# A conditioned transformer block in float32: the second norm turned through DRAM, and a planner's order that counts two engines as taking turns on a port

## Chip, core and metric

One core of one Trainium2 chip. The metric is the device time of one execution in microseconds (us), the median of several runs. The profile is one further execution, taken with the hardware profiler; times read from it are compared with its own time.

Engines are named as the profile names them: PE (TensorE, matrix products), PEld (its weight loads), DVE (VectorE), ACT (ScalarE), POOL (GpSimd) and SP (SyncE, which here only issues DMAs). Each engine works through its own instructions in the order in which they were written.

## The reference

A transformer block on x of 8 x 1024 x 512 in float32, with 16 heads of width 32 and a hidden width of 2048. Six vectors per batch row (shift, scale and gate of both halves) come from the condition.

```
mod = silu(condition) @ Wada + bada
sh_a, sc_a, gt_a, sh_m, sc_m, gt_m = split(mod, 6)
x  = x + gt_a * attention(layernorm(x, g1, be1) * (1 + sc_a) + sh_a)     # causal, with Wqkv, Wproj, bproj
xm = layernorm(x, g2, be2) * (1 + sc_m) + sh_m
x  = x + gt_m * (gelu(xm @ W1 + b1) @ W2 + b2)
```

## The kernel before

**Blocks.** The 8 x 1024 tokens are 16 blocks of 512, numbered 0 to 15: two per batch row. The queries of an even block see their own keys, those of an odd block also the keys of the block before. A block is held as four tiles of 128 tokens.

**Products.** The large products (queries, keys, values, projection, the four "up" parts of W1 and the down product of W2) are done with one Strassen level: seven products of halves in place of eight. The left or right operand of a token block is therefore kept as seven pieces: B11, B21, B22 and T1 are halves of the normed and turned block `xm`, T2, T3 and T4 are sums in a tile `t`. The sums of the weights are made once and kept in DRAM. Each product runs in four column groups of 32 on TensorE (`matmul`, L201). Weights stream in pieces of 256 KB through a ring of nine buffers, in the order in which the plan uses them (`fetch`, L336), on SP's queue. A piece can be loaded when the one nine places earlier was used up.

**The plan.** `plan[w]` (L234 to L269) lists by hand the linear steps that run beside the attention of block w: `load_xr` (x read again as the residual), `proj` (output projection of block n = w - 1, added to the residual), `mt` (second norm and its modulation), `u` (four up parts), `d` (four down parts: seven products and their additions to the residual), and for block w + 1 or w + 2 the queries, keys, values and first norm (`q`, `k`, `v`, `norm_a`, `at`). Down parts that don't fit are carried to the front of the next window in `late`. Before the change these carried parts stand ahead of `v` and `proj`.

**The planner.** While the kernel is being written down, it keeps a clock for each engine (`now`, L94) and the time at which each tile is written or free (`written`, `left`). `note` (L112) advances a clock by a fixed duration. The attention (`attend`, L1824) writes score units, exponent units and weighted sums in order; `step_aside` (L1462) fills the time until an operand is due with steps of the plan, whichever thread is due first. Nothing of this runs on the chip: it fixes the order on each engine. `either` (L154) puts an elementwise operation on VectorE or GpSimd, whichever the clocks say ends first; GpSimd is preferred by a margin of 1500 ns. `note` delays a VectorE operation marked `port` to the end of a GpSimd operation in which it would start; the other way round nothing is delayed.

**The norm.** `normalize` (L617) takes the statistics of four tiles on VectorE, the root and the application (L653) on ScalarE. Then the block is turned, so that features lie on partitions, and scaled and shifted by the modulation (`modulated`, L732). There are two ways. (1) On TensorE: sixteen transposes against the identity (L769) into three shared PSUM banks, and a scaling that reads the bank (L784 on ScalarE or L778 on VectorE). (2) Through DRAM (`turn_rows`, L702): VectorE transposes squares of 32 x 32 (L708), four DMAs write the turned squares to a DRAM tile (L719), one DMA of 1 MB reads them back (L725), and the scaling reads SBUF. `is_turned` (L376) chooses the second way for the first norm of blocks 4 to 15; x is then loaded in an order of rows that makes the tokens come out in sequence. The second norm takes the first way in all blocks.

**Lists of work in waiting.** `jobs` (statistics and square transposes on VectorE) run in sequence when their first entry is due. `transfers` (the writes and the read of a turned block) likewise, by `run_transfers` (L575). The results are stored by `store` (L1189) at once when it is called.

Of the kernel before, what the change touches and what calls it, by code (L numbers as in the profile page):

```python
# [22 lines left out]
def kernel(  # L23
# [72 lines left out]
    shape = [None]  # L96
    pool_spans = []
    NEVER = float("inf")
# [5 lines left out]
    def due(reads=(), writes=()):  # L104
# [5 lines left out]
        return t  # L110

    def note(engine, ns, reads=(), writes=(), port=False):  # L112
# [5 lines left out]
        if engine == "POOL":  # L118
            pool_spans.append((start, end))
# [31 lines left out]

    margin = [1500]

# [47 lines left out]
    def matmul(ps, lhsT, rhs, start, stop, reads=(), bank=None):  # L201

        for j in range(HPG):
            r = slice(j * hd, (j + 1) * hd)
            nc.tensor.matmul(  # L205
                ps[r, :], lhsT[:, r], rhs, start=start, stop=stop, skip_group_check=True
            )
        n = 1
        for d in rhs.shape[1:]:
            n *= d  # L210
        note_pe(2 * COLUMN * n, "columns", reads, [] if bank is None else [("l", bank)])

    MM = 853
# [26 lines left out]
    }  # L240
    late = []
    for w in range(1, NB):
        n = w - 1
        m = mlp_steps(n)
        even = blocks[n][1] == 0
        rows_a = [("rows", blocks[n][0], "a")] if even else []
        rows_m = [("rows", blocks[n][0], "m")] if even else []
        own = m[:1] + ([("load_xa", w + 2)] if w + 2 < NB else []) + m[1:3]
        own += [("norm_a", w + 2)] if w + 2 < NB else []
        if w == NB - 1:  # L250
            steps = late[:1] + [("load_xr", n)] + rows_a + [("proj", n), ("mt", n)] + late[1:]
            steps += [("v", w)] + rows_m + own + m[3:6]
            late = m[6:]
        else:
# [5 lines left out]
            at = [("at", w + 2)] if w + 2 < NB else []  # L260
            if blocks[w][1] == 0:

                late = m[3:4] + at + m[4:]
            else:
                steps += m[3:4] + at + m[4:6]
                late = m[6:]
        plan[w] = steps
    n = NB - 1
    plan[NB] = [("load_xr", n), late[0], ("beside", ("proj", n)), late[1], ("mt", n)] + mlp_steps(n)  # L269

# [103 lines left out]

    SQ = 32

    def is_turned(key):
        return key[0] == "a" and int(key[1:]) >= 4

# [181 lines left out]

    def add_job(job, reads, first=False):

        at = sum(1 for other in jobs if other[2]) if first else len(jobs)
        jobs.insert(at, (job, reads, first))

    def run_jobs(everything=False):
        while jobs and (
            everything or (now["DVE"] <= now["PE"] and due(jobs[0][1]) <= now["PE"])
        ):  # L570
            jobs.pop(0)[0]()

    transfers = []

    def run_transfers(everything=False):  # L575
        while transfers and (
            everything or max(queue_free[0], transfers[0][0]) <= now["PE"]
        ):
            ready, transfer = transfers.pop(0)
            queue_free[0] = max(queue_free[0], now["PE"], ready) + 700  # L580
            transfer()
# [25 lines left out]
    def hurry():  # L607

        while jobs and due(jobs[0][1]) <= now["PE"] + 500:
            jobs.pop(0)[0]()  # L610
        while excursions and due(excursions[0][1]) <= now["PE"] + 500:
            excursions.pop(0)[0]()
# [4 lines left out]
    def normalize(tiles, key, sources):  # L617
# [42 lines left out]
        for t in range(NTT):  # L660
            add_job(lambda t=t: statistics(t), [sources[t]], key[0] == "m")

# [39 lines left out]
    def turn_rows(key, tiles, xm):  # L702

        squares = xm.rearrange("p c (j r) -> p (c j) r", r=P)
        there = kept.tile([D, TB], F32, tag=f"turned_{int(key[1:]) % 2}", name=f"turned_{key}")

        def turn(t):
# [21 lines left out]
        for t in range(NTT):  # L729
            add_job(lambda t=t: turn(t), [("hat", key, t)])  # L730

    def modulated(key, gain, shift, b, guards):  # L732
        for t in ("B11", "B21", "B22", "T1", "T2", "T3", "T4"):
# [15 lines left out]
            "T4": sums[:, 2, :, :],  # L749
        }  # L750
        xm_of[key] = part
        at = {t: (key, t) for t in part}
# [60 lines left out]
    qTs, kTs, vs = {}, {}, {}  # L813
    projected, valued = set(), set()
    xm_of, hTs, hidden = {}, {}, set()
# [80 lines left out]
    def strassen(step, x, dest, target, row, done, put=None, after={}):  # L896
# [14 lines left out]
        def product(a, t, bank=None):  # L911
            start = bank is None
            reads = [(x, t)] + ([("sums", *step, a)] if raw and a[0] == "S" else [])
            for i in range(2):
                for k in range(2):
# [10 lines left out]
                    lhsT, rhs = (second, first) if row else (first, second)  # L926
                    matmul(
                        banks[bank][:, ts(i, HB)], lhsT[:, ts(i, P)], rhs,
                        start and i + k == 0, k == 1, reads, bank,
# [59 lines left out]
        start(tail())  # L989

    def project_T(step, store, pool, tag, done):

        n = step[1]
        dst = pool.tile([P, NC, TB], F32, tag=tag, name=f"{tag}_{n}")
        store[n] = dst
# [27 lines left out]

    residual, stored = {}, {}
    y_count, y_keys = [0], {}
# [69 lines left out]
    def project_out(n):  # L1095
# [8 lines left out]
        begun = []  # L1104

        def begin(t):

            bank = yield from accumulate(
                [(attT[:, c, ts(t, P)], piece(at[c])) for c in range(NC - 1)], [("att", n)], False
            )  # L1110
            begun.append(bank)

        for t, xt in enumerate(tiles):
            if last:
                while len(begun) <= max(t, 1):
# [3 lines left out]
                matmul(  # L1119
                    banks[bank], attT[:, NC - 1, ts(t, P)], piece(at[NC - 1]), False, True,  # L1120
                    [("att", n, t)], bank,
                )
            else:
                bank = yield from accumulate(
                    [(attT[:, c, ts(t, P)], piece(at[c])) for c in range(NC)], [("att", n)]
                )
# [62 lines left out]
    def store(n, t):  # L1189
        b, h = blocks[n]  # L1190
        for i in (2 * t, 2 * t + 1):
            r0 = h * TB + i * P
            nc.sync.dma_start(out[b, r0 : r0 + P, :], residual[n][:, i, :])
        stored[n + 1] = max(stored.get(n + 1, 0.0), due([("xr", n, 2 * t), ("xr", n, 2 * t + 1)]))

    def down(n, part):
# [19 lines left out]
        def product(operand):  # L1216
# [3 lines left out]
            for i in range(NQ):  # L1220
                p = next(at)
                for k in range(2):
                    c = 2 * i + k
                    hT = hTs[n, 2 * kh + c // NC][:, c % NC, tokens]
                    for m in range(2):
# [3 lines left out]
                        else:  # L1229
                            yield [], []  # L1230
                        matmul(
                            banks[bank][:, ts(m, HB)], hT[:, ts(m, P)], halves(p)[:, k, :],
                            c + m == 0, c == 2 * NQ - 1, reads, bank,
# [96 lines left out]
    def perform(step):  # L1330
# [12 lines left out]
        elif kind == "load_xr":  # L1343
            n = step[1]
            b, h = blocks[n]
            if n == NB - 2:
                xr = kvp.tile([P, NTT, D], F32, tag="kT", name=f"xr_{n}")
# [3 lines left out]
            for t in range(NTT):  # L1351
                r0 = h * TB + t * P
                nc.sync.dma_start(xr[:, t, :], x[b, r0 : r0 + P, :])
                landed = max(now["PE"], stored.get(n, 0.0)) + LANDING + 700 * t
                written["xr", n, t] = landed
# [15 lines left out]
        elif kind == "k":  # L1371
            yield [("free for k", step[1])], []
            yield from project_T(step, kTs, kvp, "kT", lambda: None)
        elif kind == "q":
# [449 lines left out]
    def attend():  # L1824
        previous = None
        for n in range(NB):
# [20 lines left out]
            written["free for k", n + 2 if n % 2 else n + 1] = 0.0  # L1847
            written["free for k", n + 1] = 0.0
            for g, k, n_slots, upto in slots:
                if (n, g) == groups[-1]:  # L1850
# [50 lines left out]
    def next_scores():  # L1901
        until(lambda: units[unit_at[0]][0] in projected)
        scores(*units[unit_at[0]])
# [15 lines left out]
    needs += sum(score_need(*unit) for unit in units)  # L1919
    for n in range(NB):  # L1920
        written["attended", n] = NEVER
        written["v done", n] = NEVER
# [30 lines left out]
    run_jobs(True)  # L1953
    drain()


# [46 lines left out]
```

## Time and profile before

| | |
|---|---|
| median of 3 runs | 3485.39 us (3484.59 to 3486.25) |
| the profiled execution | 3487.44 us, of it span 3485.7 us |
| granted TensorE clock, mean | 1.000 |
| matrix products of the up parts, `bank<-xm_m,w` and `bank<-t_m,w` | x8192 and x6144, mean 380 ns |
| transposes of the second norm, `bank<-ident,xh_m` (L769) | x256, mean 286 ns |
| DMA | 466.84 MB, weight queue's packets 43.8% of 16 engines' span |
| `turned_a<-xm_a` | x48, 256 KB, 4.2 us to landing |
| `xm_a<-turned_a` | x12, 1024 KB, 5.6 us to landing |

A product of this kernel leaves two records in the trace, a transpose one. A row of a group is read as: line, engine, operation, tile written <- tiles read, shape, xcount | time in which at least one of the group was running, mean ns of one | idle time of the engine just before them, and what ended it. A row of a timeline is read as: start, length, engine, line, operation, tiles, shape, xcount of merged instructions [idle time before <- who ended it]. Matrix products overlap, so the sum of the groups' times is larger than the engine's busy time; how long an instruction holds TensorE is seen from one start to the next.

### The profile page before, as it was taken

The numbers are of one execution on the slowest core, as the hardware profiler recorded it, in microseconds if no ns is written. First come the engines' busy times: TensorE is split into PE (matmuls) and PEld (weight loads), VectorE is DVE, ScalarE is ACT, GpSimd is POOL, SyncE is SP. The second block draws the span as 40 slices with busy tenths as digits, with TensorE's granted clock in tenths as the row PEclk, the third lists the DMA queues.
The fourth block names the chain that finished last, engine by engine and source line by source line (L and its number), as shares of the span: only waits on it lengthen the run. The fifth ranks groups of instructions, "written<-read, shape, count | busy, mean of one in ns | idle before, by whom it ended". The sixth has DMA issues, their size and how long they took to land.

```text
span 3485.7 us, 122756 instructions
## 1 busy us (share of the span) xinstructions
PE 3448.3 (99%) x55618; PEld 1776.1 (51%) x55618; DVE 1905.0 (55%) x2136; ACT 1286.7 (37%) x1420; POOL 2074.5 (60%) x2209
## 2 busy tenths in 40 slices
PE   8999999999999999999999999999999999999999
PEld 5544455445554554545545455454554545545445
DVE  6765664554645556465564655645546455554463
ACT  2335243352433524235152352514524244241531
POOL 3676755675466664576645766557664576644640
PEclk9999999999999999999999999999999999999999
DMA  6843334335353353633536335363443534435334
GB/s 213 271 144 86 117 110 150 120 105 172 107 167 102 105 174 104 186 95 100 173 98 186 98 111 159 101 186 98 129 140 101 183 101 135 130 100 153 90 121 136
DMA packets 350523, 466.84 MB, mean 134 GB/s; under 512 B 27460, under 2 KB 212092, under 8 KB 350004
## 3 DMA queue, kind: packets, MB, share of 16 engines
q1 hardware_dynamic: 349808, 458.73, 43.8%
q8 instruction: 438, 7.18, 0.9%
q14 instruction: 81, 0.66, 0.1%
q10 hardware_dynamic: 196, 0.28, 0.0%
HBM read 416.90 MB, written 41.99 MB: 132 GB/s over the span
## 4 chain that ended last, share of the span: by engine, by line
PE 94%; DVE 3%; POOL 1%; ACT 1%; issue 0%; DMA 0%; SPq 0%; DVEq 0%; ACTq 0%; POOLq 0%
PE bank L205 65%; PE sc L1602 9%; PE po L1736 8%; PE st L1695 7%; PE st L1683 3%; DVE mx L1619 2%; PE bank L1757 2%; PE bank L769 1%; PE bank L1657 1%; POOL pT L1821 0%; DVE sc L1616 0%; POOL mcols L1640 0%; DVE pT L1818 0%; POOL mcols L1641 0%; DMA ada<-in_L_cond_Wada_dram 0%
## 5 line engine op out<-in xcount | busy, mean ns | idle before, releaser
L1821 POOL TENSOR_TENSOR pT<-pT,pT 128x256 f32<-128x256 f32 (+3 forms) x1254 | 1174.5, 972 | 210.3 <-ACT pT L1708 119.2
L1708 ACT ACTIVATE pT<-st 128x2048 f32<-128x2048 f32 x288 | 541.1, 1879 | 1001.1 <-PE st L1695 908.8
L205 PE MATMUL bank<-w,hT 128*32 128x256 f32 x14336 | 795.5, 379 | 0.0
L1619 DVE TENSOR_REDUCE mx<-sc 128x4 f32<-128x2048 f32 (+3 forms) x384 | 665.6, 1754 | 140.3 <-PE sc L1602 133.7
L205 PEld LDWEIGHTS bank<-w,hT 128*32 128x32 f32 x14336 | 448.8, 110 | 335.6 <-issue 29.2
L205 PE MATMUL bank<-xm_m,w 128*32 128x256 f32 x8192 | 498.8, 380 | 0.0
L205 PE MATMUL bank<-t_m,w 128*32 128x256 f32 x6144 | 384.2, 380 | 0.1
L205 PEld LDWEIGHTS bank<-xm_m,w 128*32 128x32 f32 x8192 | 253.6, 110 | 238.8 <-issue 76.0
L1713 POOL TENSOR_SCALAR_AFFINE_SELECT pT<-pT 128x512 f32<-128x512 f32 x256 | 164.8, 661 | 308.8 <-ACT pT L1708 306.9
L1602 PE MATMUL sc<-kT,qT 32*128 32x512 f32 (+3 forms) x3072 | 329.1, 520 | 2.9 <-DVE mx L1619 1.9
L1616 DVE TENSOR_TENSOR sc<-sc,mask 128x1024 f32<-128x1024 f32 (+1 forms) x160 | 162.9, 1018 | 276.2 <-PE sc L1602 217.6
L1736 PE MATMUL po<-pT,v 128*32 128x512 f32 (+3 forms) x3072 | 306.0, 493 | 0.0
L1695 PE MATMUL st<-qT,kT 32*128 32x512 f32 (+3 forms) x3072 | 299.8, 486 | 0.0
L205 PEld LDWEIGHTS bank<-t_m,w 128*32 128x32 f32 x6144 | 193.0, 110 | 180.8 <-issue 54.2
L205 PE MATMUL bank<-xm_a,w 128*32 128x256 f32 x3968 | 248.8, 381 | 1.3 <-ACT xm_a L784 1.1
L197 DVE TENSOR_TENSOR hT<-bank,u_u 128x512 f32<-128x512 f32 x192 | 129.1, 686 | 151.2 <-PE bank L205 149.0
L165 POOL TENSOR_TENSOR qT<-top,rec 128x512 f32<-128x512 f32 x60 | 77.1, 1285 | 219.8 <-ACT rec L1775 219.8
L1602 PEld LDWEIGHTS sc<-kT,qT 32*128 32x128 f32 x3072 | 129.4, 183 | 150.9 <-ACT pT L1708 61.8
L205 PE MATMUL bank<-w,qT 128*32 128x256 f32 (+1 forms) x2944 | 191.4, 399 | 1.3 <-DVE qT L1782 1.3
L1153 ACT ACTIVATE hT<-hT,cols 128x512 f32<-128x512 f32 x256 | 164.2, 711 | 55.0 <-DVE hT L197 54.4
L205 PE MATMUL bank<-t_a,w 128*32 128x256 f32 x2944 | 183.3, 380 | 0.0
L165 POOL TENSOR_TENSOR hT<-hT,hT 128x1024 f32<-128x1024 f32 x28 | 79.7, 2868 | 167.6 <-DVE hT L1211 167.6
(232 smaller groups left out, 3507.5 us busy)
## 6 DMA issues: line engine op xcount, KB each, us to landing
w<-in_L_cond_W_dram SPq DMA_DIRECT2D x384, 256.0 KB, 2.9
w<-kept_up_S SPq DMA_DIRECT2D x256, 256.0 KB, 2.6
w<-kept_down_S SPq DMA_DIRECT2D x256, 256.0 KB, 2.8
w<-kept_qkv_S SPq DMA_DIRECT2D x180, 256.0 KB, 2.7
w<-in_L_cond_Wqkv_dram SPq DMA_DIRECT2D x147, 256.0 KB, 3.0
hat<-in_x_dram SPq DMA_DIRECT2D x64, 256.0 KB, 4.7
xr<-in_x_dram SPq DMA_DIRECT2D x64, 256.0 KB, 4.6
out_dram<-xr SPq DMA_DIRECT2D x64, 256.0 KB, 2.6
```

The lines of the kernel that those rows point to most:

```text
L165: nc.gpsimd.tensor_tensor(out, a, b, op)
L197: nc.vector.tensor_tensor(out, src, other, op)
L205: nc.tensor.matmul(ps[r, :], lhsT[:, r], rhs, start=start, stop=stop, skip_group_check=True)
L1153: nc.scalar.activation(hT[:, i, :], hT[:, i, :], AF.Gelu, bias=cols[:, O_B1 + f : O_B1 + f + 1])
L1602: nc.tensor.matmul(sc[:, j, c0 : c0 + w], qTs[n][r, gg, ts(qt, P)], keys_of(n, kh)[r, gg, :w], start=True, stop=True, skip_group_check=True,)
L1616: nc.vector.tensor_tensor(place, place, shape_of.to_broadcast(place.shape), ALU.add)
L1619: nc.vector.tensor_reduce(maxima[n, gg][:, kh, qt, :], sc[:, :, c0 : c0 + w], axis=AX.X, op=ALU.max)
L1695: nc.tensor.matmul(st[:, j, c0 : c0 + w], kT[r, gg, ts(k % NTT, P)], qT[r, gg, TB - w :], start=False, stop=True, skip_group_check=True,)
L1708: nc.scalar.activation(pT[:, :, :used], st[:, :, :used], AF.Exp, scale=scale)
L1713: nc.gpsimd.affine_select(diagonal, diagonal, pattern=[[0, HPG], [1, P]], compare_op=ALU.is_ge, fill=0.0, base=0, channel_multiplier=-1,)
L1736: nc.tensor.matmul(po[r, TB - w :], v[:, k % NTT, g * P + j * hd : g * P + (j + 1) * hd], pT[:, j, c0 : c0 + w], start=(k == 0), stop=last ...
L1821: nc.gpsimd.tensor_tensor(into, into, pT[:, j, c0 : c0 + w], ALU.add)
```

## The change

- **Second norm through DRAM.** `is_turned` takes blocks 3 to 13 for the second norm as well. The residual x is then read, and the result stored, with rows in another order (`row_tiles_of`): partition (a, r) of tile (h, t) holds token 256 h + 64 a + 32 t + r. The turned `xm` has its tokens in the order (a, h, n) with n of 64, so B11, B21, B22 and T1 are no longer a run of 256 columns but 4 runs of 64; T2 to T4, made from them, are a run again. `token_tile` picks the tokens of a tile from such columns for the projection and the down product.
- **Order of steps.** In windows 3 to 15 `proj` and `mt` of block n stand ahead of the down parts of block n - 1, and those ahead of the queries and keys of block w + 1. In an even window the third and fourth up part are carried to the next window.
- **Buffers.** Keys get three tiles with names of their own, and the residual of every odd block uses a key tile that is not in use.
- **Port arithmetic.** `note` records VectorE's port operations and delays GpSimd's too; `give_way` shifts GpSimd operations that were noted but start within a later VectorE operation. The margin in `either` is 1000 ns.
- **Lists.** Jobs keep their order by norm only, so that a later norm's job can pass one that is not due; transfers are taken by their time; the read back is entered when the fourth write is issued, 7000 ns later; stores are entered as transfers 1000 ns after the residual is due.

```diff
+    def give_way(start, end):
+
+        if not any(start <= a < end for a, *_ in pool_spans):
+            return
...
     def note(engine, ns, reads=(), writes=(), port=False):
         start = max(now[engine], due(reads, writes))
         if port:
-            start = max([start] + [b for a, b in pool_spans if a <= start < b])
+            start = max([start] + [b for a, b, *_ in pool_spans if a <= start < b])
+            give_way(start, start + ns - FREE)
+        elif engine == "POOL":
+            start = max([start] + [b for a, b in port_spans if a <= start < b])
...
-    margin = [1500]
+    margin = [1000]
...
+    def token_tile(columns, i, n):
+
+        if is_turned(f"m{n}"):
+            return columns.rearrange("p (a t r) -> p t a r", t=2, r=SQ)[:, i]
+        return columns[:, ts(i, P)]
...
+        if w == 1:
+            steps = head + [("k", w + 1), ("proj", n), ("mt", n), ("q", w + 1)]
+        elif w == 2:
+            steps = downs[2:] + [("v", w)] + head + [("proj", n), ("mt", n), ("q", w + 1), ("k", w + 1)]
+        elif w < NB - 1:
+            steps = late + head + [("v", w), ("proj", n), ("mt", n)] + downs + [("q", w + 1), ("k", w + 1)]
+        else:
+            steps = late + head + [("v", w), ("proj", n), ("mt", n)] + downs
...
-            steps = late + [("v", w), ("load_xr", n)] + rows_a + [("proj", n), ("k", w + 1)]
-            if w == 1:
-                steps = [("load_xr", n)] + rows_a + [("k", w + 1), ("proj", n)]
-            steps += [("mt", n), ("q", w + 1)] + rows_m + own
...
     def is_turned(key):
-        return key[0] == "a" and int(key[1:]) >= 4
+        n = int(key[1:])
+        return n >= 4 if key[0] == "a" else 3 <= n < NB - 2
...
-                transfers.append((ready + 5000, get))
 
         def put(a):
+            if a == P // SQ - 1:
+                transfers.append((queue_free[0] + 7000, get))
...
+        if rows_turned and key[0] == "m":
+            tokens = xm.rearrange("p c (a h n) -> p c h a n", h=2, n=2 * SQ)
+            part["B11"], part["T1"] = tokens[:, one, 0], tokens[:, one, 1]
+            part["B21"], part["B22"] = tokens[:, two, 0], tokens[:, two, 1]
...
     def store(n, t):
...
+        def move():
+            unstored.remove(n)
+            for i in (2 * t, 2 * t + 1):
+                nc.sync.dma_start(rows[i], residual[n][:, i, :])
+
+        transfers.append((ready + 1000, move))
```

More of the change, by code (lines that the diff above doesn't have):

```diff
@@ L110, in due @@
         return t
+    def give_way(start, end):
+        if not any(start <= a < end for a, *_ in pool_spans):
+            return
+        for i, (a, b, reads, writes) in enumerate(pool_spans):
+            if a < start:
+                continue
+            if a >= end:
+                break
+            later = end, end + b - a
+            pool_spans[i] = *later, reads, writes
+            for of, keys in ((left, reads), (written, writes)):
+                for k in keys:
+                    if of.get(k) == b + SYNC:
+                        of[k] = later[1] + SYNC
+            end = later[1]
+        now["POOL"] = max(now["POOL"], end)
     def note(engine, ns, reads=(), writes=(), port=False):
@@ L240 @@
     }
-    late = []
+    late, downs = [], []
     for w in range(1, NB):
@@ L560, with add_job, next_job @@
     jobs = []
-    def add_job(job, reads, first=False):
-        at = sum(1 for other in jobs if other[2]) if first else len(jobs)
-        jobs.insert(at, (job, reads, first))
-    def run_jobs(everything=False):
[L568 to L571, printed above, removed]
+    def add_job(job, reads, line, first=False):
+        at = sum(1 for other in jobs if other[3]) if first else len(jobs)
+        jobs.insert(at, (job, reads, line, first))
+    def next_job(by):
+        passed = set()
+        for i, (_, reads, line, _) in enumerate(jobs):
+            if line not in passed and due(reads) <= by:
+                return i
+            passed.add(line)
+        return None
+    def run_jobs(everything=False):
+        while jobs:
+            i = 0
+            if not everything:
+                i = next_job(now["PE"]) if now["DVE"] <= now["PE"] else None
+            if i is None:
+                return
+            jobs.pop(i)[0]()
     transfers = []
     def run_transfers(everything=False):
[L576 to L579, printed above, removed]
+        while transfers:
+            i = min(range(len(transfers)), key=lambda i: transfers[i][0])
+            if not everything and max(queue_free[0], transfers[i][0]) > now["PE"]:
+                return
+            ready, transfer = transfers.pop(i)
             queue_free[0] = max(queue_free[0], now["PE"], ready) + 700
@@ L1190, in store, with stored_by @@
         b, h = blocks[n]
[L1191 to L1194, printed above, removed]
+        rows = row_tiles_of(out[b, h * TB : (h + 1) * TB, :], n)
+        ready = due([("xr", n, 2 * t), ("xr", n, 2 * t + 1)])
+        stored[n + 1] = max(stored.get(n + 1, 0.0), ready)
+        unstored.append(n)
+        def move():
[3 more added lines that the diff above has]
+        transfers.append((ready + 1000, move))
+    def stored_by(n):
+        while n in unstored:
+            run_transfers(True)
     def down(n, part):
@@ L1350, in perform @@
             residual[n] = xr
[L1351 to L1354, printed above, removed]
+            for t, rows in enumerate(row_tiles_of(x[b, h * TB : (h + 1) * TB, :], n)):
+                nc.sync.dma_start(xr[:, t, :], rows)
+                landed = max(now["PE"], stored.get(n - 1, 0.0)) + LANDING + 700 * t
                 written["xr", n, t] = landed
@@ L1920 @@
     for n in range(NB):
+        written["free for xr", n] = 0.0 if n == NB - 1 else NEVER
         written["attended", n] = NEVER
```

104 lines of the change are left out of this document (67 added, 37 removed).

## The prediction

> **What bounds the kernel now.** I read the busy times first, then the chain that ended last, then the busy time by stage, then TensorE's own waits.
>
> ```profile
> span 3485.7 us, 122756 instructions
> PE 3448.3 (99%) x55618; PEld 1776.1 (51%) x55618; DVE 1905.0 (55%) x2136; ACT 1286.7 (37%) x1420; POOL 2074.5 (60%) x2209
> PE 94%; DVE 3%; POOL 1%; ACT 1%; issue 0%; DMA 0%; SPq 0%; DVEq 0%; ACTq 0%; POOLq 0%
> ```
> ```profile
> core 0: us, PE busy (x) PEld busy (x) DVE busy (x) ACT busy (x) POOL busy (x), PEclk, DMA share, GB/s
> 0.00:65.00 65.00, 50.99 (x784) 33.38 (x784) 38.69 (x62) 15.36 (x23) 21.86 (x30) 0.97 0.75 247
> 800.00:3110.00 2310.00, 2302.55 (x37500) 1186.24 (x37496) 1246.74 (x1390) 861.35 (x949) 1411.92 (x1503) 1.00 0.44 131
> 3330.00:3486.00 156.00, 148.28 (x2516) 82.71 (x2508) 81.82 (x107) 32.35 (x49) 35.52 (x24) 1.00 0.45 135
> ```
>
> The reader is to see that TensorE has work in 3448.3 of 3485.7 us, and that the 37.4 us without lie mostly at the ends: 14.0 in the first 65 us and 7.7 in the last 156. In the long middle, from 800 to 3110 us, where the eleven changed blocks stand, it idles for 7.45 us. The other engines are at 37 to 60%. So the time is what TensorE is given to do. An edit gains by taking products from it; an edit to another engine gains next to nothing and costs only if TensorE comes to wait for it.
>
> **The change part by part.**
>
> *1. The turn of the second norm leaves TensorE (blocks 3 to 13).* Sixteen 128x128 transposes for each of 11 blocks go, 176 in all. Nothing else on TensorE changes in kind or count: in the two orders all other products agree, and the groups of row-tiled and column-tiled products alternate as often as before (576 and 590 runs, against 576 and 591). The transposes' row in the middle stage, and what stood around them:
>
> ```profile
> L769 PE MATMUL bank<-ident,xh_m 128*128 128x128 f32 x176 | 28.6, 286 | 1.5 <-ACT xm_m L784 1.5
> ...
> 1528.61 1.48 PE L205 MATMUL bank<-t_a,w 128*32 128x256 f32 x24
> 1530.01 0.66 PE L769 MATMUL bank<-ident,xh_m 128*128 128x128 f32 x4
> 1530.60 0.64 PE L205 MATMUL bank<-t_a,w 128*32 128x256 f32 x8
> 1531.54 0.33 PE L769 MATMUL bank<-ident,xh_m 128*128 128x128 f32 x1 [0.30 <-ACT xm_m L784]
> ```
>
> The 28.6 us are a union of overlapping records. From start to start four transposes hold TensorE for 1530.60 - 1530.01 = 0.59 us, so 44 fours are 26.0 us, and the waits in front of them, 1.5 us, go too: **-27.5 us**. The upper bound is the whole row, 28.6 + 1.5 = 30.1. The lower takes the one latency of 0.286 out of each four's 0.66: 0.374/3 = 0.125 apiece, 22 us. I take the middle, which is read from the neighbours' starts.
>
> [...]
>
> *2. What takes its place.* Four square transposes on VectorE, four writes to DRAM and one read back per block, and a scaling that reads SBUF. The first norm already goes this way, so its round trip is in the trace:
>
> ```profile
> 1641.00 2.91 ACT L653 ACTIVATE hat<-hat,offset_a,rstd_a 128x512 f32<-128x512 f32 x4
> ...
> 1668.05 2.93 ACT L784 ACTIVATE xm_a<-xm_a,shifta,gaina 128x512 f32<-128x512 f32 x4 [16.53 <-DMA xm_a<-turned_a]
> ```
> ```profile
> 1647.42 1.89 DVE L708 STREAM_TRANSPOSE xm_a<-hat 128x512 f32<-128x512 f32 x3
> ...
> 1650.70 0.70 DVE L708 STREAM_TRANSPOSE xm_a<-hat 128x512 f32<-128x512 f32 x1
> ...
> 1671.74 0.69 DVE L162 TENSOR_TENSOR t_a<-xm_a,t_a 128x512 f32<-128x512 f32 x1
> ```
>
> From the last square transpose (1651.4) to the scaling is 16.65 us; from the end of the norm (1643.9) to the last operand (1672.4) 28.5. The 44 VectorE transposes are 44 x 0.683 (mean of the 48 there) = 30 us, on an engine that is 55% busy. ScalarE stood 16.53 us at the landing, yet TensorE shows no wait there:
>
> ```profile
> 1650.07 25.22 PE L205 MATMUL bank<-w,hT 128*32 128x256 f32 x464
> ```
>
> The weight queue carries 2 MiB more per block, about 23 MB on 467. It has 44 writes and 11 reads more; the reads wait for their writes at the head of SyncE's queue, with weight loads behind. TensorE waits for no weight load today, with 12 such round trips. I cost it at nothing.
>
> *3. Projection and norm in front of the older down parts.* This moves no product's cost, only what covers what. Cover before: the norm of a block has its queries or keys behind it, and the chain is
>
> ```profile
> 1721.87 0.68 DVE L197 TENSOR_TENSOR y<-bank,u_proj 128x512 f32<-128x512 f32 x1
> ...
> 1750.15 2.92 ACT L653 ACTIVATE xh_m<-xr,offset_m,rstd_m 128x512 f32<-128x512 f32 x4
> ```
>
> 31.2 us from the last projection copy to the end of the norm; with the round trip's 28.5 it is 60 us. In the new order TensorE has four down parts and both projections for queries and keys between a block's projection and its first up product, with attention woven in:
>
> ```profile
> L205 PE MATMUL bank<-w,hT 128*32 128x256 f32 x14336 | 795.5, 379 | 0.0
> ```
>
> 795.5/16 = 49.7 us of down products per block, and a projection of queries or keys has a quarter of their records, 12.4 us: 74.6 without attention. Counted over the printed order with each form's pitch, the distance is 82 to 114 us for blocks 3 to 13, against 41 to 47 before. If the cover were gone, a block would lose 60 us less what stays; with 22 us to spare I cost it at nothing. The price is paid at the front: from the end of a block's attention to its projection there were 55 to 92 us of products and now there are 27 to 42. The chain there (logarithm, copy, exponent, product, first difference) is under 5 us by its rows of 0.57 to 1.3, so that too is nothing.
>
> *4. Strided operands.* In a turned block tokens stand as 4 runs of 64 columns. Four of seven operands of each up projection read so: 4 x 32 records x 4 x 11 = 5632 records of about 55 ns, 310 us. No row shows a TensorE operand in runs. The nearest rows cut 512 columns into two instructions:
>
> ```profile
> 1699.19 1.03 PE L1695 MATMUL st<-qT,kT 32*128 32x256 f32 x16
> 1700.15 1.07 PE L1736 MATMUL po<-pT,v 128*32 128x384 f32 x16
> ...
> 1707.34 1.03 PE L1695 MATMUL st<-qT,kT 32*128 32x512 f32 x8
> 1708.29 0.64 PE L1736 MATMUL po<-pT,v 128*32 128x256 f32 x8
> ...
> 1723.17 1.09 PE L1695 MATMUL st<-qT,kT 32*128 32x384 f32 x16
> 1724.19 0.41 PE L1657 MATMUL bank<-ident_b,mcols 128*32 128x128 bf16 x16
> ```
>
> Whole: 0.95 us to the next start; halves 0.96; 384 and 128 1.02. So 8 cuts cost 0.01 to 0.07 us, 1.25 to 8.8 ns each. Three seams in 5632 records would be 21 to 148 us if a seam cost as much as a new instruction. A gain is excluded, for the columns are the same. I take 0: VectorE's square transposes, written in runs of 32, take 0.683 against 0.69 for the plain rows of that size. For the range I keep the even cut's bound.
>
> [...]
>
> *5. Port arithmetic and deferred stores.* The planner now sends 46 of the 47 large differences of the down operands that GpSimd had to VectorE, and some small ones:
>
> ```profile
> L165 POOL TENSOR_TENSOR hT<-hT,hT 128x1024 f32<-128x1024 f32 x28 | 79.7, 2868 | 167.6 <-DVE hT L1211 167.6
> L165 POOL TENSOR_TENSOR hT<-hT 128x1024 f32<-128x1024 f32 x19 | 57.5, 3038 | 0.0
> L1211 DVE TENSOR_TENSOR hT<-hT 128x1024 f32<-128x1024 f32 x32 | 38.8, 1252 | 0.0
> L162 DVE TENSOR_TENSOR y_d<-y_d,row_gm 128x512 f32<-128x512 f32 x16 | 29.7, 1858 | 0.3
> ```
>
> GpSimd loses about 137 us of these, VectorE gains 46 x 1.25 = 58 us; with the transposes and a few small ones it comes to some 2000 us in 3458, 58%. The row of 1.86 us, against 0.69 for the plain form, shows the two taking turns. Off the path on both sides: nothing, with the middle's 7.45 us of idle (1.5 of it counted in part 1) as the most it can win.
>
> *Sum.* Profiled execution 3487.4 (span 3485.7 and 1.7 around it) - 27.5 = 3459.9. The shown runs' median is 2.05 us under that execution, so 3485.4 - 27.5 = **3458**. By the bounds of part 1 3455 to 3463.
>
> **The rivals.**
>
> *A: a late round trip stops ScalarE.* The scaling waits for the read at the head of ScalarE's queue; behind it in blocks 4 to 12 (even) stand exponents, in the odd ones copies of query and key banks. For an even block the order gives 30.1 us of products from the score tile that VectorE reduces last before its square transposes to the exponent group behind. The chain is about 3.5 + 2.7 + 16.65 + 2.93 = 25.8, so 4.3 us are to spare. SyncE's weight loads stand in its way for up to 5.55 us at a time:
>
> ```profile
> 1664.13 5.55 SPq L346 DMA_DIRECT2D w<-in_L_cond_W_dram  x4
> ...
> DMA to landing us min/median/max: 3.2/4.4/7.3
> ```
>
> and a write lands up to 2.9 us over its median: 8.4 - 4.3 = 4.1 us late, five blocks, 20 us: **3478**. Against it: the twelve trips of today leave no trace on TensorE, though those fall in stretches without attention.
>
> *B: the seams cost.* One mechanism: the moving operand loses time at each run's end. At 1.6 ns a seam (27.5 us over 16,896 seams) the gain is gone; above 2.1 ns the kernel is slower by over 0.2%. At the uneven cut's 8.8 ns: 3458 + 148 = **3606**. For it only the uneven cut; against it the even one, at 1.25.
>
> *C: the new arithmetic misjudges the port,* so the planner does not do what it says: VectorE takes 46 large operations and copies that TensorE's banks wait for come late. The longest wait for VectorE in the middle:
>
> ```profile
> PE sc L1602 <- DVE mx L1619: 1.4, 6, 0.5
> ```
>
> 46 x 0.5 = 23 us: **3481**, no change that can be told. For it the 58% and the fixed durations in the planner; against it that VectorE idles in four tenths of the span.
>
> **How the numbers follow.** Forecast 0.72, A 0.16, B 0.05, C 0.07. The low end takes part 1's upper bound and 3 us of the other waits: 3485.4 - 30.1 - 3 = 3452. The high end takes the even cut's term up to 17 of its 21 us, which is also most of A: 3475. A measurement of this kernel tells 0.2%, 7 us, from no change. Faster by more: forecast and nearly all of A, 0.87. Within: C and the rest of A, 0.08. Slower: B, 0.05.
>
> **What would show it.** Right: transposes on the identity down to 80 for this norm, TensorE busy near 3421 us with its idle near 37, 44 writes and 11 reads more, 256-column up products still at 380 ns. A shows as TensorE waiting for ScalarE's exponents in even blocks; B as a longer mean of the up products alone; C as waits for VectorE's copies or maxima. I am wrong if TensorE's idle grows by over 15 us or its other products get longer.

## The result, and the profile after

| | kernel before | changed kernel |
|---|---|---|
| median of the runs (us) | 3485.2 (5 runs, 3484.6 to 3486.3) | 3470.9 (5 runs, 3469.0 to 3472.8) |
| ratio to before, 95% interval | | 0.9961 (0.9949 to 0.9972) |
| profiled execution (us) | 3487.4 | 3470.9 |

The change wins 14.3 us, and the time is 12.9 us above the forecast's 3458. The runs below stand beside the kernel before at 3484.2 to 3485.1. First the page of the changed kernel: span, busy times, chain that ended last.

```profile
span 3469.2 us, 122474 instructions
PE 3423.4 (99%) x55442; PEld 1778.0 (51%) x55442; DVE 2055.4 (59%) x2262; ACT 1301.4 (38%) x1444; POOL 1944.2 (56%) x2101
PE 89%; DVE 4%; DMA 4%; ACT 1%; issue 1%; POOL 1%; SPq 0%; DVEq 0%; ACTq 0%; POOLq 0%
```

TensorE's busy time fell by 24.9 us, but its idle time rose from 37.4 to 45.8, and the chain goes through DMAs for 4% of the span, where it was 0%. The busy time by stage (the middle ends 15 us earlier now) says where:

```profile
0.00:65.00 65.00, 50.89 (x804) 33.89 (x808) 40.32 (x64) 15.68 (x24) 22.74 (x33) 1.00 0.76 249
800.00:3095.00 2295.00, 2275.98 (x37295) 1183.65 (x37288) 1361.36 (x1488) 877.44 (x977) 1297.41 (x1404) 1.00 0.49 142
3313.00:3469.00 156.00, 152.00 (x2652) 87.02 (x2644) 74.75 (x106) 25.87 (x47) 18.64 (x13) 1.00 0.48 145
```

In the middle TensorE idles for 19.0 us in place of 7.45. The groups of the changed kernel, each shape apart (busy, mean ns, idle before and its releaser):

```profile
L233 PE MATMUL bank<-xm_m,w 128*32 128x256 f32 x8192 | 500.7, 381 | 4.6 <-DVE xm_m L841 4.5
L832 PE MATMUL bank<-ident,xh_m 128*128 128x128 f32 x80 | 11.7, 283 | 0.8 <-ACT xm_m L847 0.4 <-ACT xh_m L709 0.4
```

The transposes went from 256 to 80, and the products of the row with the strided operands (5632 of its 8192) take 381 ns. Next come lines of TensorE's list of waits (us in total, times, longest). The first, for VectorE's maxima, was 2.4 us before; the others are new, two of them for weights and one, the second, with a transfer behind it:

```profile
PE st L1773 <- DVE mx L1709: 7.5, 12, 1.9
PE bank L233 <- DVE xm_m L841: 4.5, 1, 4.5
PE bank L233 <- DMA w<-in_L_cond_Wproj_dram: 3.2, 2, 1.6
PE bank L233 <- DMA w<-kept_proj_S: 2.3, 4, 0.8
```

The kernel before had no wait of TensorE for a weight load in its middle. What stands behind the 4.5 us is in SyncE's timeline of block 5 (the last write of the round trip, four stores, the read), and in the chain there:

```profile
1299.40 0.76 SPq L776 DMA_DIRECT2D turned_m<-xm_m  x1
1300.26 1.97 SPq L1276 DMA_DIRECT2D out_dram<-xr  x2
...
1304.55 2.15 SPq L1276 DMA_DIRECT2D out_dram<-xr  x2
...
1310.71 1.18 SPq L782 DMA_DIRECT2D xm_m<-turned_m  x1
```
```profile
1310.71 11.04 DMA xm_m<-turned_m
```

The read of the turned norm takes 11.04 us, where the reads of the first norm's trips take 5.5 (median, by their completions) and the other ten of the second norm 5.3 to 7.3, and four stores of a residual were issued ahead of it. The list of transfers (count, KB each, median us to landing) gives the residual's rows before; for the changed kernel it gives these rows without a landing time:

```profile
xr<-in_x_dram SPq DMA_DIRECT2D x64, 256.0 KB, 4.6
out_dram<-xr SPq DMA_DIRECT2D x64, 256.0 KB, 2.6
```

The trace's completion events, matched to their transfers, tell why. Four loads of one block in each kernel (issue; number of completions; when after the issue, in us):

```
before   2327.7  16   2.5 ... 4.3
         2328.1  16   3.3 ... 5.2
         2328.6  16   3.5 ... 5.4
         2329.1  16   3.9 ... 5.5
changed  2903.5   5   1.0  4.9  5.3  5.5  5.7
         2904.2   5   1.0  7.4  7.8  8.1  8.4
         2904.8   5   0.9 10.6 11.3 11.5 12.0
         2905.4   5   1.2 13.1 13.8 13.9 14.4
```

A load of the turned row order ends with one early completion and four late ones. Issued 0.6 us apart, such loads end 3.0 to 4.2 us apart, as if they queued for the same few DMA engines. The busy share of the 16 DMA engines says the same. For 3 us in which only these four loads run (first row) it is a quarter, at 94 GB/s; while the four of the kernel before land (second row) it is 0.92, at 322 (the last two numbers of a row):

```profile
2906.00:2909.00 3.00, 3.00 (x76) 1.88 (x71) 0.69 (x1) 1.07 (x2) 0.00 (x0) 1.00 0.25 94
2331.00:2334.00 3.00, 3.00 (x52) 1.45 (x48) 0.32 (x1) 0.00 (x0) 0.00 (x0) 1.00 0.92 322
```

The first projection weights behind the four loads are issued at 2906.2 us and land at 2920.2, right after the last of them (2919.8). Over the whole trace the residual's loads land in 8.7 us (median; 4.5 before), its stores in 7.0 (2.7), and the sums of the projection weights (`w<-kept_proj_S`) in 10.4 (3.7). These medians still contain the blocks that aren't turned; the 44 loads and 44 stores of the turned blocks alone take 11.4 and 8.8.

The slowest dimension of the new row order is 4, and four of the five completions come late. The first norm's loads of x in blocks 4 to 15, with 32 rows outermost, have 16 completions each in both kernels, as the residual's loads and stores of before have. That the count of the slowest dimension sets on how many engines a transfer is put was my theory here; the runs with 32, 16 and 8 outermost, below, test it.

### The profile page after: what moved, and what is told of

It is laid out like the page before. It is cut to its first block, busy times and chain, and to the rows that moved or that the text cites. A ratio compares the mean times of both kernels' runs of the same rounds, so it can differ in the third digit from the quotient of the medians.

```text
span 3469.2 us, 122474 instructions
## 1 busy us (share of the span) xinstructions
PE 3423.4 (99%) x55442; PEld 1778.0 (51%) x55442; DVE 2055.4 (59%) x2262; ACT 1301.4 (38%) x1444; POOL 1944.2 (56%) x2101
## 4 chain that ended last, share of the span: by engine, by line
PE 89%; DVE 4%; DMA 4%; ACT 1%; issue 1%; POOL 1%; SPq 0%; DVEq 0%; ACTq 0%; POOLq 0%
PE bank L233 62%; PE sc L1692 8%; PE po L1826 7%; PE st L1785 7%; PE st L1773 3%; DVE mx L1709 2%; DMA w<-kept_proj_S 2%; PE bank L1847 2%; DMA w<-in_L_cond_Wproj_dram 1%; DVE sc L1706 1%; ACT pT L1798 1%; DMA xm_m<-turned_m 1%; PE bank L1747 0%; DVE hT L1299 0%; DMA xr<-in_x_dram 0%
## 5 line engine op out<-in xcount | busy, mean ns | idle before, releaser
L1911 POOL TENSOR_TENSOR pT<-pT,pT 128x256 f32<-128x256 f32 (+3 forms) x1254 | 1213.5, 1003 | 143.1 <-ACT pT L1798 112.3
L233 PE MATMUL bank<-w,hT 128*32 128x256 f32 x14336 | 814.1, 380 | 0.0
L1803 POOL TENSOR_SCALAR_AFFINE_SELECT pT<-pT 128x512 f32<-128x512 f32 x256 | 177.1, 710 | 436.8 <-ACT pT L1798 431.5
L233 PE MATMUL bank<-xm_a,w 128*32 128x256 f32 x3968 | 239.3, 380 | 2.4 <-ACT xm_a L847 1.1
L233 PEld LDWEIGHTS bank<-xm_a,w 128*32 128x32 f32 x3968 | 127.7, 110 | 97.4 <-issue 13.9
```

What stands on the lines that cost most here:

```text
L233: nc.tensor.matmul(ps[r], columns, rhs, start=start, stop=stop, skip_group_check=True)
L1803: nc.gpsimd.affine_select(diagonal, diagonal, pattern=[[0, HPG], [1, P]], compare_op=ALU.is_ge, fill=0.0, base=0, channel_multiplier=-1,)
L1911: nc.gpsimd.tensor_tensor(into, into, pT[:, j, c0 : c0 + w], ALU.add)
```

## The experiments

Each kernel was timed in several rounds beside the kernel before.

**The residual in parts of 32 rows.** The turned blocks' loads and stores keep their row order and are cut the other way, so that the slowest dimension is 32; a block then has eight loads of 128 KB in place of four of 256, and as many stores. The stores (the loads likewise):

```diff
+        parts = rows.rearrange("(h a t r) d -> a r h t d", h=2, t=2, r=SQ)
+        return [parts[a] for a in range(P // SQ)]
...
+                for a in range(P // SQ):
+                    mine = residual[n][a * SQ : (a + 1) * SQ, 2 * t : 2 * t + 2, :]
+                    nc.sync.dma_start(parts[a][:, t], mine)
```

> The changed kernel, with the residual of the turned blocks 3 to 13 loaded and stored by 32 rows and two token tiles at a time (8 loads and 8 stores per block in place of 4 and 4); the orders of TensorE, VectorE, ScalarE and GpSimd are those of the changed kernel. In the changed kernel a residual load or store of a turned block is finished by 5 completions instead of 16 and lands in 8.7 and 7.0 us (medians), where those of the kernel before took 4.5 and 2.7. Theory (the permuted rows put each such transfer on few of the 16 DMA engines, and the weight loads and the read of the round trip that follow on the queue come late): the residual lands in 3 to 5 us again, the stalls within runs of like 256-column products fall from 17.6 us to about 4, TensorE's idle from 45.8 to about 37, and the time to 3458 to 3461. Rival 1 (the 2 MiB more per block, or the round trip itself, makes the weight loads late): 3470, the stalls stay. Rival 2 (the new order and the port arithmetic cost 13 us): 3470 too, with the waits for VectorE's maxima and for banks that the changed kernel has.

Measured 3458.8 us (3458.0 to 3459.0), ratio 0.9925 (0.9913 to 0.9938): 12.2 us under the changed kernel, and the forecast's number. The page, then one group of products:

```profile
span 3456.8 us, 122657 instructions
PE 3421.4 (99%) x55442; PEld 1778.2 (51%) x55442; DVE 2051.7 (59%) x2262; ACT 1300.9 (38%) x1444; POOL 1944.0 (56%) x2101
PE 92%; DVE 4%; ACT 2%; issue 1%; DMA 0%; POOL 0%; SPq 0%; DVEq 0%; ACTq 0%; POOLq 0%
w<-kept_proj_S SPq DMA_DIRECT2D x56, 256.0 KB, 4.2
```
```profile
L233 PE MATMUL bank<-xm_m,w 128*32 128x256 f32 x8192 | 499.2, 380 | 0.5 <-issue 0.4
```

TensorE idles for 35.4 us, the DMAs are off the chain, and the projection weights land in 4.2 us. By their completions, 16 each, the 88 loads and 88 stores land in 4.8 and 3.4. What went adds up: the waits of 4.5, 3.2 and 2.3 us above make 10.0 of the 10.4 us by which the idle time fell, and with 2.0 us of busy time 12.0. The 44 writes and 11 reads of the round trip are all still there, so rival 1 falls; the order and the arithmetic too, so rival 2 falls.

> As the first, but only the residual's loads are cut into 32 rows; the stores stay as in the changed kernel. Theory: the waits for weight loads right behind the residual's loads go (projection weights, 3.2 + 2.3 us on TensorE, and what of the stalls of 1 us and less hangs on them), the 4.5 us wait for the read of the turned norm in block 5, with four stores ahead of it, stays: 3462 to 3466. Rivals: 3470.

> As the first, but only the stores are cut into 32 rows; the loads stay. Theory: the 4.5 us wait of block 5 goes and little else, 3465 to 3467; together with the loads alone the gains add up to those of both. Rivals: 3470.

Loads alone: 3467.6 us (3464.3 to 3470.3); stores alone: 3465.2 (3464.6 to 3468.0). By the medians the two win 3.4 and 5.7, together 9.1 of the 12.2; by the profiled executions 6.6 and 6.2. The first lies above its expected 3462 to 3466, and its runs spread over 6 us, so the split is no finer than that, and that the two gains add up isn't shown. The places are as expected. With the loads even, the waits for projection weights are gone and block 5's is not; with the stores even it is the other way round:

```profile
PE bank L233 <- DVE xm_m L848: 4.6, 1, 4.6
```
```profile
PE bank L233 <- DMA w<-in_L_cond_Wproj_dram: 3.4, 2, 1.9
PE bank L233 <- DMA w<-kept_proj_S: 2.4, 4, 0.9
```

**The row order alone, in the kernel before.**

```diff
+        if 3 <= n < NB - 2:
+            tiles = rows.rearrange("(h a t r) d -> h t a r d", h=2, t=2, r=32)
+            return [tiles[i // 2, i % 2] for i in range(NTT)]
```

> The kernel before with nothing changed but the rows of these transfers: the residual of blocks 3 to 13 is loaded and stored in the turned blocks' row order (four runs of 32 rows per tile), while all else stays in plain order, so that each token's residual is that of another token. Theory: the residual's transfers land in 7 to 9 us as in the changed kernel, weight loads behind them come later, and the time goes from 3485 to between 3488 and 3498, depending on how near the weight loads behind them were to TensorE's need. Rivals 1 and 2: 3485, since neither the traffic nor the order is changed.

Measured 3539.8 us, ratio 1.0157 (1.0143 to 1.0171): the direction of the theory, and over four times the most that I gave it (54.9 us, against 13). TensorE's longest new wait, the chain at one of its five places, and VectorE's timeline there:

```profile
PE bank L205 <- DVE y L197: 32.6, 5, 6.8
```
```profile
1474.93 11.46 DMA out_dram<-xr
...
1489.04 13.40 DMA row_ga<-kept_ga
```
```profile
1502.46 0.69 DVE L197 TENSOR_TENSOR y<-bank,row_ga 128x512 f32<-128x512 f32 x1 [8.50 <-DMA row_ga<-kept_ga]
```

In the order of before, the gate's row is loaded behind four residual loads, which stand behind the stores; it lands 13.40 us after its issue, and the projection's banks wait for it. Weight loads, which the expectation named, cost less: TensorE's waits for `w<-in_L_cond_Wqkv_dram` are 6.5 us. The changed kernel issues the rows in front of the residual and has no such wait; whether that alone makes the difference between 55 and 12 us wasn't tried. TensorE's busy time grew by 13.0 us too, with the same instructions, at a mean granted clock of 0.995 in place of 1.000 (below).

> As the run of the kernel before with four runs of 32 rows per tile (3539.8 us), but each tile's rows are 16 runs of 8; the residual again is that of other tokens. Theory (the outermost count of the transfer's rows sets on how many of the 16 DMA engines it is put): 16 completions that matter, landing as in the kernel before (4.5 and 2.7 us), time 3483 to 3490. Rival 3 (rows out of order are slow in themselves, in DRAM): as slow as with runs of 32 rows, 3530 to 3550.

> As the one with 16 runs of 8 rows, but 8 runs of 16 per tile; the residual again is that of other tokens. Theory: the transfer goes over 8 engines, its landing is between (4 to 6 us for a load, 3.5 to 5 for a store); the stalls behind it shrink by more than half, because most of the time was lost where a load came later than its slack: 3487 to 3515. Rival 3: 3530 to 3550.

16 runs: 3484.9 us, ratio 1.0002 (0.9993 to 1.0010); 8 runs: 3484.5, 1.0001 (0.9992 to 1.0010). Rival 3 falls: rows out of order cost no time. With 16 runs every transfer has 16 completions, and loads and stores land in 5.1 and 3.1 us (medians). Size and number of the transfers are those of the kernel before here, so it isn't the smaller parts of the first experiment that help. With 8 runs a load of the reordered blocks has 9, one early and eight late, and lands in 6.5 us (median of the 44; 9.8 with 4 runs), a store in 6.3 (9.3). The completions, 9 for 8 runs and 16 for 16, beside the changed kernel's 5 for 4, fit the theory; the engines' busy share was read for 4 alone. The landings with 8 runs are slower than expected, yet no time is lost, against my 3487 to 3515. So in the kernel before, loads and stores of 6.5 and 6.3 us cost nothing, and of 9.8 and 9.3 they cost 55 us: what counts is whether the lateness passes the slack of what waits behind.

**The turn taken out, the rest of the change kept.**

```diff
-        return n >= 4 if key[0] == "a" else 3 <= n < NB - 2
+        return n >= 4 if key[0] == "a" else False
```

> The changed kernel with the second norm of every block turned on TensorE and the tokens in plain order, as before; its order of steps, port arithmetic and deferred stores are kept. It has the 256 transposes of the kernel before and residual transfers in plain rows with 16 completions. If order, arithmetic and deferral are worth nothing, as forecast: 3482 to 3489. Rival 2 (they cost the 13 us that were missing): 3495 to 3500. Each microsecond that this run is above 3485 is what the new order costs, each below is what it wins, and the turn's own gain is then the distance to the 3458.8 of the kernel with 32-row transfers.

Measured 3484.5 us (11 runs), ratio 1.0003 (0.9994 to 1.0012). Order, arithmetic and deferral together are worth nothing by themselves (between 2 us won and 4 lost), and the turn, with even transfers, is worth 3484.5 - 3458.8 = 25.7 us.

**The arithmetic and the margin put back, with the turn and even transfers.** Both back:

```diff
-            give_way(start, start + ns - FREE)
-        elif engine == "POOL":
-            start = max([start] + [b for a, b in port_spans if a <= start < b])
...
-    margin = [1000]
+    margin = [1500]
```

> The kernel with all residual transfers by 32 rows (3458.8 us), with the planner's port arithmetic of before: no giving way of GpSimd's operations, no spans of VectorE's, margin 1500. Large differences of the down operands go back to GpSimd. If the arithmetic is worth nothing, as forecast: 3455 to 3463. If the new arithmetic wins: above 3463. If it costs (the waits for VectorE's maxima went from 2.4 + 1.9 to 7.5 + 1.6 us): 3452 to 3455.

Measured 3476.6 us (3475.0 to 3480.4): 17.9 us of the gain are gone. TensorE's first waits, then a group of GpSimd's:

```profile
PE st L1787 <- DVE mx L1723: 16.9, 23, 1.7
PE bank L1761 <- POOL mcols L1745: 11.0, 9, 1.6
```
```profile
L184 POOL TENSOR_TENSOR hT<-hT,hT 128x1024 f32<-128x1024 f32 x26 | 68.6, 2657 | 17.0 <-DVE hT L1306 17.0
```

Of the large differences 34 are back on GpSimd, where the new arithmetic leaves 1. The maxima that TensorE needs come later (16.9 us of waits, 7.5 with the new arithmetic), and GpSimd's columns of them too (11.0, 5.9).

The margin alone:

> The kernel with all residual transfers by 32 rows (3458.8 us) with the change's port arithmetic kept and only the margin put back from 1000 to 1500 ns. The run with both put back took 3476.6 us, TensorE waiting 16.9 us for VectorE's maxima in place of 7.5. If the arithmetic of the turns on the port is what keeps VectorE in time: 3456 to 3463, with the maxima's wait under 10 us. If the margin is: 3470 to 3480, with the maxima's wait near 17 us.

Measured 3471.7 us (3470.9 to 3472.7): 12.9 us lost, with the wait for the maxima at 13.1. So the margin carries most of it, and the spans and the giving way some 5 (3476.6 - 3471.7), in this order; the arithmetic put back with the new margin kept wasn't run. The time is the one expected of the margin, the wait for the maxima lies between the two. 22 of the large differences are on GpSimd, and TensorE also waits 5.5 us for ScalarE's exponents (0.2 with even transfers alone).

**The stores at once.**

```diff
-        transfers.append((ready + 1000, move))
+        move()
```

> The kernel with all residual transfers by 32 rows (3458.8 us), with each store issued where it was in the kernel before, right after the additions are given out, in place of 1 us after the planner's time for the last of them. Only SyncE's order changes. If the deferral is worth nothing, as forecast: 3455 to 3463, with SyncE standing 60 to 100 us at the stores for GpSimd's and VectorE's additions (85.9 us in the kernel before). If it is what keeps the weight loads in time: 3465 and more, with waits of TensorE for weights behind the stores.

Measured 3512.7 us, ratio 1.0080 (1.0067 to 1.0093): 53.9 us lost, and not by the weights. TensorE's two new waits and SyncE's at the stores, then the timeline of one place of five, in order of time: SyncE's last write, stores and read, ScalarE, TensorE.

```profile
PE bank L233 <- ACT p_q L217: 29.0, 5, 6.3
PE sc L1712 <- ACT pT L1818: 7.8, 5, 4.8
SPq L1289 <- POOL xr L190: 87.7, 20, 8.4
```
```profile
1725.20 0.98 SPq L783 DMA_DIRECT2D turned_m<-xm_m  x1
...
1738.21 1.77 SPq L1289 DMA_DIRECT2D out_dram<-xr  x4
1740.03 0.44 SPq L789 DMA_DIRECT2D xm_m<-turned_m  x1
...
1745.91 2.93 ACT L854 ACTIVATE xm_m<-xm_m,shiftm,gainm 128x512 f32<-128x512 f32 x4 [23.11 <-DMA xm_m<-turned_m]
1748.74 0.56 ACT L217 COPY p_q<-bank 128x512 f32<-128x512 f32 x1
...
1749.36 3.21 PE L233 MATMUL bank<-xm_a,w 128*32 128x256 f32 x28 [5.65 <-ACT p_q L217]
```

The stores wait at the head of SyncE's queue for the last additions, and the read stands behind them: 14.8 us pass from the last write's issue to the read's. ScalarE stands 23.11 us at the scaling, the copy of a query bank behind it is late, and TensorE waits 5.65 us for the bank. With the stores deferred, the same read goes out 8.6 us after the last write, ahead of the stores, and ScalarE's 16.96 us reach nobody:

```profile
1706.87 0.98 SPq L783 DMA_DIRECT2D turned_m<-xm_m  x1
1715.49 0.39 SPq L789 DMA_DIRECT2D xm_m<-turned_m  x1
1722.44 2.16 SPq L1289 DMA_DIRECT2D out_dram<-xr  x4
...
1721.36 2.93 ACT L854 ACTIVATE xm_m<-xm_m,shiftm,gainm 128x512 f32<-128x512 f32 x4 [16.96 <-DMA xm_m<-turned_m]
```

**More blocks turned.** The rule's bounds become 3 to 14, or 2 to 13.

> The kernel with all residual transfers by 32 rows, with the second norm of block 14 turned through DRAM too (blocks 3 to 14). 16 transposes more leave TensorE, 2.5 us by the forecast's 0.59 us for four; four down parts and attention still stand behind its projection: 3455 to 3458. If the block's norm is late with no queries or keys of a later block behind it: up to 10 us slower, 3460 to 3470, with TensorE's wait for the first operand of the up products at 3200 to 3300 us.

> The kernel with all residual transfers by 32 rows, with the second norm of block 2 turned through DRAM too (blocks 2 to 13). 16 transposes less, 2.5 us: 3455 to 3458. Block 2's projection stands in front of queries and keys with two down parts in between as in the later even blocks; if the stretch, in which the weights' sums are still being made, has no room on VectorE or the queue: 3459 to 3465.

Measured 3460.1 us (3458.2 to 3463.2) and 3457.9 (3457.5 to 3459.2), beside 3458.8 (3458.0 to 3459.0). Neither can be told from the kernel with even transfers, and the first lies above its expected 3455 to 3458. In its profile TensorE's busy time is 1.5 us longer than with even transfers, though 16 transposes are gone; its clock stands at one half for two stretches of 6.83 us, where the kernel with even transfers has one of 3.41 (the end of the span left out in both). In the profile of the second the busy time falls by 2.1 us and the idle time grows by 1.5. The version to keep is the changed kernel with its residual in parts of 32 rows, 26 us under the kernel before.

## Why the prediction was wrong in size

*1. The turn leaves TensorE, -27.5: right.* 256 to 80 transposes; the kernel without the turn and the one with it and with even transfers are 25.7 us apart, and TensorE's busy time ended at 3421.4 where 3421 was forecast. The reading by starts was the good one: the mean of 286 ns, taken as time held, would have been an estimated 50 us (176 x 0.286).

*2. What takes its place, "44 writes and 11 reads more … I cost it at nothing": here is the step that failed.* The sentence counted the round trip's own transfers and left out the 44 loads and 44 stores of the residual, whose access pattern the same change rewrites in the function for the rows of a tile. Their bytes and count are those of before, so I gave them no term at all. In the turned blocks they take 11.4 and 8.8 us to land in place of 4.5 and 2.7, and weights and the round trip's read queue behind them: 12.2 us, of the 12.9 missing. The reason I gave, that twelve round trips leave no wait for weights today, held and said nothing about these transfers. The diff showed the pattern, and the kernel before held the contrast: its rows for the first norm are loaded as `x[b, r0 : r0 + P, :].rearrange("(t r) d -> r t d", r=SQ)`, with 32 rows outermost.

*3. Projection and norm in front, nothing: right* as far as the whole goes (1.0003 without the turn). The order also moved the gate's row in front of the residual's loads, which I did not price; the run of 3539.8 us shows what such a row can cost when it stands behind them, five waits of up to 6.8 us.

*4. Strided operands, nothing: right.* 381 ns in the changed kernel, 380 with even transfers, 380 before. Rival B falls with it.

*5. Port arithmetic and deferred stores, nothing: right against the kernel before, and wrong about what they cover.* I asked what they win by themselves, and not what the turn would cost without them: 17.9 us without the new arithmetic and margin, 53.9 without the deferral. C's sign is there all the same: the waits for VectorE's maxima grew from 2.4 to 7.5 us, with even transfers too, though the idle time as a whole fell from 37.4 to 35.4 there. And VectorE's large differences grew by 100 us (101 to 201), not by 58, for one of them now takes 1.37 to 1.93 us and not 1.25. Waits of the kind that rivals A and C describe do arise, at those prices, when parts of the change are put back. A stopped the odd blocks' copies of query banks (29.0 us) more than the even ones' exponents (7.8), and stores, not weight loads, stood in the read's way.

The rivals as I priced them: none was the cause. 3470.9 lies between the forecast and A's 3478, but TensorE hardly waited for exponents (0.8 us). A's price also rested on a misread line: the 7.3 us are the longest landing of writes and reads together, and by their completions the writes take 5.6 at most, 1.4 over their median. A would then have been 5.55 + 1.4 - 4.3 = 2.7 us at five places, 3471, which is the measured time by chance and not by its mechanism. That the time lies inside the range is luck too, for the high end was made of the strided term, which came out as nothing. My own sign for being wrong, idle time grown by over 15 us, was not reached: it grew by 8.4, and 2.0 of the loss sat in busy time, of which the low clock behind block 5's wait explains at most 1.4 (below).

## What to carry to other kernels

When a change reorders rows, write out the access pattern of every transfer that follows the new order, and read its slowest dimension: here, at the same bytes and the same count, 4 rows outermost left 5 completions and a busy share of the DMA engines of 0.25, where plain rows had 16 and 0.92. Check the number of completions of a transfer in the trace, not only its bytes. And price each part of a change twice: what it wins alone, and what the other parts would lose without it.

## What was not expected of the hardware

Two waits of TensorE cost more than their length. The windows around block 5's wait in the changed kernel, and around one of the stalls with the stores at once (in each row the third number from the end is the granted clock):

```profile
1317.00:1323.00 6.00, 1.52 (x28) 0.63 (x24) 1.19 (x3) 0.82 (x1) 0.00 (x0) 0.97 0.83 282
1323.00:1327.00 4.00, 3.79 (x44) 1.90 (x40) 3.65 (x6) 0.59 (x1) 1.78 (x1) 0.62 0.10 36
```
```profile
1748.00:1754.00 6.00, 4.64 (x44) 2.17 (x48) 2.14 (x4) 1.89 (x4) 1.78 (x1) 0.52 0.49 181
1754.00:1760.00 6.00, 6.00 (x108) 3.28 (x104) 2.06 (x3) 0.00 (x0) 0.00 (x0) 0.91 0.51 130
```

After 4.5 us without work the clock was 0.62 for the next 4 us: 0.38 of 3.79 us busy, an estimated 1.4 us lost on top. After 5.65 us it was 0.52 and then 0.91: 0.48 x 4.64 + 0.09 x 6 = 2.8 us, an estimate too. The trace's record of the clock has it at one half for 3.41 us from 1322.6 on, and for 6.83 us from 1748.2 on. The run with the stores at once shows the sum: 29.0 and 7.8 us of waits for ScalarE and 16.9 us more of busy time are 53.7 of the 57.1 us by which its profiled span is longer than with the stores deferred (3513.9 against 3456.8). What makes the second stretch twice as long as the first isn't shown.
